# Layer 3 of a four-layer graph-attention kernel: the output additions read a PSUM tile only when it is whole, and the planner has new ranks

## The chip, the cores and the metric

The kernel runs on one core of one Trainium2 chip. The metric is the device time of one execution in microseconds, here the median over several runs of the same program. The work is spread over five engines that run side by side and meet only through semaphores: PE (TensorE, matrix products), DVE (VectorE), ACT (ScalarE), POOL (GpSimd), and SP (SyncE), which issues nearly all transfers.

## The reference, cut to what matters

The input `x` holds 128 graphs of 64 nodes with 512 features, in float32, and `adj` is one 64x64 adjacency mask per graph. Four layers follow each other, each with its own layernorm, a ReLU and a residual:

```python
h = jnp.maximum(_layernorm(x, axis=-1), 0.0)
x = x + _L0_gnn_ref(h, adj, ...)     # and L1, L2: masked attention, 4, 8 and 4 heads
h = jnp.maximum(_layernorm(x, axis=-1), 0.0)
x = x + _L3_gnn_ref(h, adj, ...)     # layer 3, below
```

Layer 3 is another kind of attention, with 8 heads of 64:

```python
m = embs @ map_w.T + map_b                        # "map"
n = sem / norm                                    # rows of m, per head, scaled to length 1
cos_adj = (cos(n, n) * (~sm) > 0.1)
q = m @ q_w.T + q_b ;  k = m @ k_w.T + k_b
p_attn = softmax(where(sm, NEG, q k^T / 8)) * keep
adj = cos_adj * p_attn
sem_h = embs @ gcn_map_w.T + gcn_map_b            # gcn_W is folded into this product ("sem")
out = relu(adj @ sem_h @ gcn_W.T / (adj.sum(-1) + 1))
```

So each output element is the larger of zero and a weighted sum, plus the residual `x`.

## The kernel before, in words

**Tiling.** The 8192 rows of `x` are cut into 16 steps `s` of 512 tokens, which are 8 graphs. Each layer goes over the 16 steps. A product of a 512x512 weight with the 512 tokens of a step is done by a scheme with seven half-size products instead of eight (`winograd`, L789 on, calls `product`, whose matmul is L741). It uses three PSUM tiles in turn, called mA, mB and mC in the profile: mA from one ring of two tiles, mB and mC from another ring of two, which the squared lengths (`mmn`) use as well. ACT reads the first value out of a tile (L758, L762 with a bias, L778) and DVE adds a later one (L771, L782).

**Layer 3, one step.** Four such products are made: `map`, `sem`, `q` and `k`. Beside them there are four blocks of small 64x64 matmuls or of a 32-column product: the scores `sc` (L1090), the cosines `cos` (also L1090), the weighted sums `po` (L1475) and the squared lengths `mmn` (L1033). `sc`, `cos` and `po` each take two PSUM tiles of two banks, called u = 0 and u = 1, and all come from one ring of two such tiles (`r_sc`). A tile is handed on only when all of its readers are done. On the way from `sc` to `po`, DVE masks the scores (L1100), takes the maximum (L1106), subtracts it (L1116); ACT takes the exponential (L1119); DVE sums rows (L1126), makes a 0/1 mask of the cosines (L1428) and multiplies (L1437); POOL divides (L1135); ACT copies 32x32 blocks (L1144) and DVE transposes (L1148). The squares that `mmn` sums are made by ACT (L1028), and the sums are read by DVE (L1013).

**The end of a step.** `last` (L1447 on) issues the `po` matmuls: for each u, first half b = 0 and then half b = 1 of the tile, 16 matmuls each in the source. `finish` (L1342) is the other side: for each half, DVE reads 256 columns out of both banks of the tile, takes the maximum with zero and adds the residual tile `xres` in one instruction (L1349). Then SP stores the sums (L1361; L1356 in the last step). The residual tiles were loaded before (L1334) into a ring of three. In the kernel before, `finish` is started ahead of the matmuls of its tile, and two events (`halves`) tell it that a half is written.

**What sets the order.** Nothing is ordered by hand. A planner (`Order.run`) runs all parts as coroutines against assumed durations, such as `dve(0.69)`, and writes each instruction into its engine's queue when it comes up: the stream that can start first is taken, and among equal starts the one with the lower rank. The ranks come from the table `RANK`, one number for each kind of work and layer; rank 0 is reserved for reading out PSUM tiles, which may also hold back another operation on DVE or ACT that would be in their way. On the chip every engine works through its own queue in the order that the planner wrote. Dependencies between engines are set as the instructions are written, and for PSUM they go by whole banks: a matmul written behind a DVE read of the same bank waits for that read, even if it goes to other columns.

**What else the change touches.** `norms` uses a small tile `rn` for the reciprocal lengths, in a pool with one buffer.

Of the kernel before, what the change touches and what calls it, by code (L numbers as in the profile page):

```python
# [8 lines left out]
F32 = mybir.dt.float32  # L9
# [5 lines left out]
P = 128  # L15
# [16 lines left out]
LEAD = [(0, 0), (0, 1)]  # L32

RANK = {
    "lead": (0.3, 1.5, 5.5, 5),
    "load": (4, 5.5, 1.5, 2),
    "norm0": (1.5, 3.5, 3.5, 6.5),
    "norm1": (4.5, 2.5, 1, 4),
    "move": (6.5, 4.5, 6, 0.3),
    "turn": (1.5, 1, 6, 3.5),  # L40
    "part": (3.5, 3.5, 4, 6),
    "weight": (5.5, 4.5, 5.5, 2.5),
    "proj": (6.5, 5, 5, 6),
    "out": (3.5, 5, 5, 3),
    "front": (2, 3, 0.5, 3),
    "soft": (1.5, 1.5, 0.3, 1),
    "near": (2, 2, 2, 2),
    "trans": (3.5, 1, 0.5, 2),
    "att": (2.5, 0.5, 2, 2),
    "res": (5.5, 6, 1.5, 5.5),  # L50
    "msum": (4.5, 4.5, 4.5, 4.5),
    "length": (4.5, 3.5, 1.5, 5),
}


# [4 lines left out]
def rank(what, l):  # L60

    return Rank(RANK[what][l])
# [28 lines left out]
class Stream:  # L91
# [14 lines left out]
    def quads(self):  # L106
        return self.op[3:] == ("quads",)
# [115 lines left out]
def pe(us):  # L223
    return ("pe", us, 0.25)
# [6 lines left out]
def dve(us):  # L231
    return ("dve", us, 0.1)


def act(us):
    return ("act", us, 0.1)


def pool(us):
    return ("pool", us, 0.15)  # L240


def load(us=2.2):
    return ("sp", 0.6, us)
# [3 lines left out]
def gnn_stack(ctx: ExitStack, tc: tile.TileContext, a: dict, out: bass.AP):  # L248
# [3 lines left out]
    od = Order()  # L252
# [10 lines left out]
    small = ctx.enter_context(tc.tile_pool(name="small", bufs=4))  # L263
    soft = ctx.enter_context(tc.tile_pool(name="soft", bufs=3))
# [617 lines left out]
    st, p_ready, s_ready, p_used, pt_done, o_used, turn = {}, {}, {}, {}, {}, [], []  # L882
# [110 lines left out]
    def sums_after(e, B, z, done, last):  # L993
        yield e

        T, z["T_done"] = yield from (r_w if last else r_t).new("mT_T")
        t2, z["t2_done"] = yield from r_t2.new("mT_T2")
        z["T"] = T = [T[:, 0], T[:, 1], t2, T[:, 2]]
        done.set()
        yield from sums_of_b(B, T, z["T_made"])  # L1000
# [10 lines left out]
    def lengths_out(ss, p_, pe_, done):  # L1011
        yield dve(0.69)
        nc.vector.tensor_copy(ss, p_)  # L1013
        pe_.set()
        done.set()

    def norms(mT, s, m_ready, ready, used):

        yield m_ready
        if s == 0:  # L1020
            yield o_done
        elif s < NG - 1:
            yield lengths[s - 1]
        sqs = []
        for c in range(NC):
            sq, e = yield from r_u.new("sq")
            yield act(0.63)
            nc.scalar.activation(sq, mT[:, c, :], AF.Square)  # L1028
            sqs.append((sq, e))
        p_, pe_ = yield from r_mm.new("mmn")  # L1030
        for c in range(NC):
            yield pe(0.24)
            nc.tensor.matmul(p_[32 * c:32 * (c + 1), :], sel, sqs[c][0], start=True, stop=True)  # L1033
            sqs[c][1].set()
        ss, se = yield from r_u.new("ss")
        copied = od.event()
        od.spawn(lengths_out(ss, p_, pe_, copied), 0)
        yield copied
        d = [dram.tile([8, TB * P], F32, name=f"{n}{s}") for n in ("ss", "rs")]
        yield ("sp", 2.4, 2.2)  # L1040
        for c in range(NC):
            nc.sync.dma_start(d[0][2 * c:2 * c + 2, :], ss[32 * c:32 * c + 2, :])
        se.set()
        if s == NG - 1:
            squares.set()

        rs = small.tile([P, 32], F32, tag="rn", name="rn", bufs=1)
        yield load(2.2)
        nc.sync.dma_start(rs, d[0].rearrange("h (k n) -> (h k) n", n=32))

        yield dve(0.2)
        nc.vector.tensor_scalar_max(rs, rs, 1e-16)
        yield pool(6.0)
        nc.gpsimd.tensor_tensor(rs, rs, mhalf[:, 0:1].to_broadcast([P, 32]), ALU.pow)
        yield load(2.2)
        nc.sync.dma_start(d[1].rearrange("h (k n) -> (h k) n", n=32), rs)
        nr = []

        if s == NG - 2:
            yield squares  # L1060
        for c in range(NC):
            t, e = yield from r_u.new("nr")
            yield ("sp", 1.3, 3.1)
            for par in range(2):
                v = d[1][2 * c + par:2 * c + par + 1, :]
                nc.sync.dma_start(t[par * N:(par + 1) * N, :],
                                  bass.AP(tensor=v.tensor, offset=v.offset,
                                          ap=[[0, N], [1, TB * P]]))
            nr.append((t, e))
        yield used  # L1070
        for c in range(NC):
            t, e = nr[c]
            yield pool(1.3)
            nc.gpsimd.tensor_mul(mT[:, c, :], mT[:, c, :], t)
            e.set()
        ready.set()
# [251 lines left out]
    def last_residuals(s, got):  # L1328
        for u in range(2):
            v, e = yield from r_xres.new()  # L1330
            x3 = v.rearrange("p b (g e) -> p (b g) e", g=2)
            for s2 in range(2):
                yield load(2.8)
                nc.sync.dma_start(x3[s2 * N:(s2 + 1) * N], by_half(x_of(3, s), 2 * u, s2))  # L1334
            got[u] = (x3, e)
            got["e", u].set()

    def by_half(x, t, s2):

        return x[t * P:(t + 2) * P, s2 * H:(s2 + 1) * H].rearrange("(i n) e -> n i e", n=N)  # L1340

    def finish(s, u, po, poe, got, halves):  # L1342
        yield got["e", u]
        x3, xe = got[u]
        for b in range(2):
            yield halves[b]
            v = x3[:, 2 * b:2 * b + 2, :]
            yield dve(0.69)
            nc.vector.scalar_tensor_tensor(v, po[:, :, b * H:(b + 1) * H], 0.0, v,  # L1349
                                           ALU.max, ALU.add)  # L1350
            if s == NG - 1:
                for s2 in range(2):
                    yield load(2.8)
                    q = slice(s2 * H, (s2 + 1) * H)
                    o = out[(s * TB + 2 * u + b) * P:(s * TB + 2 * u + b + 1) * P, q]
                    nc.sync.dma_start(o.rearrange("(i n) e -> n i e", n=N),  # L1356
                                      v[s2 * N:(s2 + 1) * N])
        poe.set()
        for s2 in range(2 if s < NG - 1 else 0):
            yield load(2.8)  # L1360
            nc.sync.dma_start(by_half(out[s * TB * P:(s + 1) * TB * P, :], 2 * u, s2),  # L1361
                              x3[s2 * N:(s2 + 1) * N])
        xe.set()
# [83 lines left out]
    def last(s):  # L1447
        z = st[3, s]
        got = {("e", u): od.event() for u in range(2)}
        od.spawn(last_residuals(s, got), rank("res", 3))  # L1450
        yield p_ready[3, s]
        room = []
        if s < NG - 1:
            for u in range(2):
                yield z["pt_ready", u]
            for u in range(2):
                room.append((yield from r_sc.new("po3")))
        for u in range(2):
            if s == NG - 1:
                yield z["pt_ready", u]  # L1460
                room.append((yield from r_sc.new("po3")))
            pt, pte = z["pt", u]
            po, poe = room[u]
            halves = [od.event() for _ in range(2)]
            od.spawn(finish(s, u, po, poe, got, halves), 0)
            for b in range(2):
                t = 2 * u + b
                for i in range(4):
                    yield quads(0.121)
                    for ch in range(2):  # L1470
                        h = 4 * ch + i
                        c, par = h // 2, h % 2
                        for g in range(2):
                            r = slice(g * N, (g + 1) * N)
                            nc.tensor.matmul(  # L1475
                                po[ch * N:(ch + 1) * N, g, (4 * b + i) * N:(4 * b + i + 1) * N],
                                pt[r, 8 * par + 2 * c + b, :],
                                z["v"][r, t, h * N:(h + 1) * N], start=True, stop=True)
                halves[b].set()
            pte.set()  # L1480
            if u == 1:
                z["v_done"].set()

    def fronts(steps):
        for l, s in steps:
            yield rank("front", l)
            yield from front(l, s)
# [88 lines left out]
```

## Time and profile before

| | before |
|---|---|
| median of 3 runs | 2678.22 us (2678.01 to 2680.61) |
| profiled execution | 2674.79 us |
| its span, first to last instruction | 2673.0 us |
| PE busy | 2629.7 us, 98% of the span |
| DVE, ACT, POOL busy | 72%, 71%, 60% of the span |
| granted PE clock | 0.998 |
| from the first `po` block (1855.63 us) to the end of the span | 817.4 us |

The profile is of one execution, and the runs are of others, so a sum of durations is made against 2673.0 us and then carried over to the median. PE is busy almost throughout, so what counts is what PE waits for and in which stretch. The times of rows in a timeline are microseconds from the start of the span. One float32 matmul of the source is two records of PE: the 32 matmuls of a `po` tile are 64 records, and a block of two tiles is 128.

### The profile page before, as it was taken

What the parts mean: (1) busy time and instruction counts of PE and PEld (TensorE: products, weight loads), DVE (VectorE), ACT (ScalarE), POOL (GpSimd) and SP (SyncE); (2) the same over time, 40 slices, a digit from 0 to 9 for tenths busy, and PEclk for the clock granted to TensorE, in tenths of its full rate; (3) what the DMA queues carried; (4) which work ended last, traced back from release to release, by engine and by line L of the source; (5) the groups of instructions that cost most, each with busy time, mean ns of one, the idle gap of its engine ahead of it and who ended that gap; (6) DMA issues with size and microseconds to landing.
All of it is one profiled execution on the core that took longest, in us unless ns stands there. A gap on an engine that the chain in (4) does not pass through costs nothing.

```text
span 2673.0 us, 64016 instructions
## 1 busy us (share of the span) xinstructions
PE 2629.7 (98%) x26352; PEld 2308.0 (86%) x26352; DVE 1918.9 (72%) x2843; ACT 1890.3 (71%) x3508; POOL 1608.8 (60%) x1246
## 2 busy tenths in 40 slices
PE   8999999999999999999999999999999999999998
PEld 7888988888888888888899999888888888888887
DVE  6877878876677667758767777658666677766667
ACT  5677777888777877876667777766676666677654
POOL 5776767554444435445767777786665566565563
PEclk9999999999999999999999999999999999999999
DMA  6666663221122112115656666332223332222231
GB/s 177 154 168 144 175 146 118 93 96 49 49 65 80 49 55 75 64 49 129 162 130 177 152 168 160 118 103 66 66 68 83 95 79 66 66 65 74 75 82 48
DMA packets 414004, 270.02 MB, mean 101 GB/s; under 512 B 277520, under 2 KB 322576, under 8 KB 413712
## 3 DMA queue, kind: packets, MB, share of 16 engines
q1 hardware_dynamic: 402048, 254.40, 35.0%
q10 hardware_dynamic: 11664, 11.54, 1.4%
q8 instruction: 207, 3.39, 0.5%
q14 instruction: 85, 0.70, 0.1%
HBM read 166.77 MB, written 67.63 MB: 88 GB/s over the span
## 4 chain that ended last, share of the span: by engine, by line
PE 92%; DVE 3%; DMA 2%; issue 1%; SPq 1%; ACT 1%; POOL 1%; POOLq 0%; DVEq 0%
PE mA L741 47%; PE mC L741 24%; PE mB L741 12%; PE sc L1090 3%; PE po L1295 2%; DMA xin<-x 1%; PE cos L1090 1%; PE po L1475 1%; SPq L1361 1%; PE mmn L1033 1%; DVE xres L1349 1%; PE mP L741 1%; DVE sc L1100 0%; POOL v L1006 0%; PE ptr L688 0%
## 5 line engine op out<-in xcount | busy, mean ns | idle before, releaser
L1144 ACT COPY F<-E 32x512 f32<-32x512 f32 x752 | 462.5, 615 | 37.5 <-POOL E L1135 25.6
L1232 POOL TENSOR_TENSOR xres<-xres,u 128x512 f32<-128x512 f32 x192 | 253.0, 1323 | 352.4 <-ACT u L1227 289.5
L515 ACT ACTIVATE xin<-xin,rs 128x512 f32<-128x512 f32 x320 | 248.8, 810 | 11.5 <-DVE rs L508 9.3
L1211 POOL TENSOR_TENSOR xres<-xres,u 128x512 f32<-128x512 f32 x192 | 249.8, 1319 | 5.6 <-DVE qk L782 4.1
L611 ACT COPY hT<-xin 32x512 f32<-32x512 f32 x390 | 240.1, 616 | 6.5
L497 DVE BATCH_NORM_STATS2 st<-xin 128x6 f32<-128x512 f32 x320 | 213.0, 668 | 40.9 <-DMA xin<-x 33.2
L506 POOL TENSOR_TENSOR rs<-rs,mhalf 128x2 f32<-128x2 f32 x160 | 120.1, 751 | 171.9 <-DVE rs L504 157.1
L758 ACT COPY v<-mA 128x256 f32<-128x256 f32 (+1 forms) x192 | 92.0, 479 | 131.6 <-PE mA L741 124.2
L385 POOL TENSOR_TENSOR t<-hT,t 128x512 f32<-128x512 f32 x126 | 178.4, 1416 | 4.8
L1126 DVE TENSOR_REDUCE sm<-E 128x16 f32<-128x1024 f32 x124 | 149.6, 1206 | 18.4 <-ACT E L1112 15.1
L1135 POOL TENSOR_TENSOR E<-E,sm 128x1024 f32<-128x1024 f32 x64 | 122.5, 1920 | 61.3 <-DVE sm L1130 42.1
L385 POOL TENSOR_TENSOR t<-hT 128x512 f32<-128x512 f32 x63 | 82.9, 1316 | 123.7 <-DVE hT L621 111.6
L1100 DVE COPY_PREDICATED sc<-n,negs 128x1024 f32<-128x1024 uint8 x64 | 99.8, 1559 | 57.5 <-PE sc L1090 57.2
L1148 DVE STREAM_TRANSPOSE F<-F 128x1024 f32<-128x1024 f32 x94 | 116.2, 1236 | 29.1 <-ACT F L1144 29.0
L741 PE MATMUL mA<-w_vo,t 128*128 128x128 f32 (+1 forms) x768 | 135.2, 312 | 1.5 <-ACT v L758 1.0
L1112 ACT ACTIVATE E<-sc,mx 128x64 f32<-128x64 f32 x512 | 123.9, 332 | 17.1 <-DVE mx L1109 17.0
L1227 ACT COPY u<-mA 128x512 f32<-128x512 f32 x144 | 84.4, 586 | 64.3 <-PE mA L741 55.8
L741 PE MATMUL mA<-hT,w_qk 128*128 128x256 f32 x496 | 126.1, 382 | 3.3 <-DVE hT L662 3.1
L1135 POOL TENSOR_TENSOR E<-E,f 128x1024 f32<-128x1024 f32 x30 | 61.1, 2036 | 104.9 <-DVE nz L1180 57.2
L741 PEld LDWEIGHTS mA<-w_vo,t 128*128 128x128 f32 x768 | 112.8, 191 | 11.4 <-ACT v L758 1.2
L741 PE MATMUL mA<-t,w_qk 128*128 128x256 f32 x496 | 119.7, 379 | 0.0
L1106 DVE TENSOR_REDUCE mx<-sc 128x16 f32<-128x1024 f32 x96 | 116.9, 1218 | 2.5
(236 smaller groups left out, 7341.4 us busy)
## 6 DMA issues: line engine op xcount, KB each, us to landing
x<-xres SPq DMA_DIRECT2D x96, 512.0 KB
xin<-x SPq DMA_DIRECT2D x96, 512.0 KB
xres<-x SPq DMA_DIRECT2D x64, 512.0 KB
F<-xin SPq DMA_DIRECT2D x480, 64.0 KB
xres<-in_x SPq DMA_DIRECT2D x32, 512.0 KB
u<-rs SPq DMA_DIRECT2D x128, 128.0 KB
xres<-x SPq DMA_DIRECT2D x64, 256.0 KB
xin<-in_x SPq DMA_DIRECT2D x30, 512.0 KB
```

The costliest lines, as they stand in the source:

```text
L385: nc.gpsimd.tensor_tensor(o, i0, i1, ALU.subtract)
L497: nc.vector.bn_stats(st, v[:, t, :])
L506: nc.gpsimd.tensor_tensor(rs[:, 0, :], rs[:, 1, :], mhalf[:, :2], ALU.pow)
L515: nc.scalar.activation(v[:, t, :], v[:, t, :], func, bias=rs[:, 2, t:t + 1], scale=rs[:, 0, t:t + 1])
L611: nc.scalar.copy(o, v)
L741: nc.tensor.matmul(o, l, r, start=(first and m == 0 and k == 0), stop=(k == KC - 1), skip_group_check=True)
L1112: nc.scalar.activation(E[:, i, :], S3[:, i, :], AF.Exp, bias=mx[:, i:i + 1], scale=0.125)
L1126: nc.vector.tensor_reduce(o, E, AX.X, ALU.add)
L1135: (nc.vector if vector else nc.gpsimd).tensor_mul(E, E, sm[:, :, None].to_broadcast([P, 16, N]))
L1144: nc.scalar.copy(F[g * N + 32 * k:g * N + 32 * (k + 1), :, 32 * i:32 * (i + 1)], E[g * N + 32 * i:g * N + 32 * (i + 1), :, 32 * k:32 * (k ...
L1211: nc.gpsimd.tensor_add(xr[:, t, :], xr[:, t, :], bo[l])
L1232: nc.gpsimd.tensor_add(v, v, both(u))
```

## The change

Three edits are made.

1. In `last`, `finish` is started after the matmuls of its whole tile, not before them, and the two `halves` events are gone. The four additions (L1348 in the changed kernel) and the stores (L1360, L1355) are the same instructions as before.
2. Most numbers of `RANK` are new.
3. The pool of `rn` has two buffers.

```diff
 RANK = {
-    "lead": (0.3, 1.5, 5.5, 5),
-    "load": (4, 5.5, 1.5, 2),
-    "norm0": (1.5, 3.5, 3.5, 6.5),
+    "lead": (0.5, 1, 5.5, 5),
+    "load": (2.5, 4, 4.5, 2),
+    "norm0": (1.5, 3.5, 4, 6.5),
     "norm1": (4.5, 2.5, 1, 4),
-    "move": (6.5, 4.5, 6, 0.3),
-    "turn": (1.5, 1, 6, 3.5),
-    "part": (3.5, 3.5, 4, 6),
-    "weight": (5.5, 4.5, 5.5, 2.5),
-    "proj": (6.5, 5, 5, 6),
-    "out": (3.5, 5, 5, 3),
-    "front": (2, 3, 0.5, 3),
-    "soft": (1.5, 1.5, 0.3, 1),
-    "near": (2, 2, 2, 2),
-    "trans": (3.5, 1, 0.5, 2),
-    "att": (2.5, 0.5, 2, 2),
-    "res": (5.5, 6, 1.5, 5.5),
-    "msum": (4.5, 4.5, 4.5, 4.5),
-    "length": (4.5, 3.5, 1.5, 5),
+    "move": (2.5, 4.5, 6, 4.5),
+    "turn": (0.5, 1, 6, 3.5),
+    "part": (2, 3, 2.5, 6),
+    "weight": (6, 4.5, 3, 2),
+    "proj": (5.5, 5, 5, 6),
+    "out": (4.5, 5, 5, 6.5),
+    "front": (2, 4, 0.5, 3),
+    "soft": (1.5, 2.5, 0.3, 4.5),
+    "near": (2, 5.5, 4.5, 2),
+    "trans": (3.5, 1, 0.5, 1),
+    "att": (2.5, 2, 1.5, 6),
+    "res": (4.5, 6, 2, 5.5),
+    "msum": (1.5, 1.5, 1.5, 1.5),
+    "length": (3, 3.5, 6.5, 5.5),
 }
...
-        rs = small.tile([P, 32], F32, tag="rn", name="rn", bufs=1)
+        rs = small.tile([P, 32], F32, tag="rn", name="rn", bufs=2)
...
-    def finish(s, u, po, poe, got, halves):
+    def finish(s, u, po, poe, got):
         yield got["e", u]
         x3, xe = got[u]
         for b in range(2):
-            yield halves[b]
             v = x3[:, 2 * b:2 * b + 2, :]
             yield dve(0.69)
...
             po, poe = room[u]
-            halves = [od.event() for _ in range(2)]
-            od.spawn(finish(s, u, po, poe, got, halves), 0)
             for b in range(2):
...
-                halves[b].set()
             pte.set()
             if u == 1:
                 z["v_done"].set()
+            od.spawn(finish(s, u, po, poe, got), 0)
```

What the planner makes of it can be read from the order of the built programs. On PE the two programs are the same in layers 0 to 2 and in layer 3 up to and with the first block of `po`. From there on, in a step of the steady part (`q` and `k` below belong to one step, and `map` and `sem` to the next):

```
before:  q x7  k x4  po  k x3  map x1 (3 of 4)  sc  map x7  sem x1 (2 of 4)  cos  sem x2  mmn  sem x5
after:   q x7  k x7  po  map x2 (1 of 4)  sc  map x6  sem x3 (2 of 4)  cos  sem x1  mmn  sem x4
```

Here "x4" means four of the seven half-size products, and "(3 of 4)" tells after which matmul of a product the small block cuts in; the number behind it counts the rest of that product as one. Around these, ACT, DVE, POOL and SP have another order in layer 3: after `sc`, ACT reads mC of `map` (L762) before the first exponential (L1119), where it came behind it; DVE takes the statistics of the next input (L497) behind the first masked and subtracted tile, where they came before it; the two halves of the next input (L569) are each loaded behind one pair of output stores, where both came behind all four; POOL normalises `m` (L1074) in one run of four. In layers 0 to 2 a few neighbours change places on DVE, ACT, POOL and SP.

## The prediction

> **What bounds the kernel now.** I read the page's busy times and chain first, then PE's waits, then one steady step of layer 3 on PE and on the engines that PE waits for.
>
> ```profile
> PE 2629.7 (98%) x26352; PEld 2308.0 (86%) x26352; DVE 1918.9 (72%) x2843; ACT 1890.3 (71%) x3508; POOL 1608.8 (60%) x1246
> ...
> PE 92%; DVE 3%; DMA 2%; issue 1%; SPq 1%; ACT 1%; POOL 1%; POOLq 0%; DVEq 0%
> ```
>
> PE is the bound; the amount of PE work does not change, so only PE's idle time can be won or lost. The list of what PE waits for (total, times, longest) says where it is:
>
> ```profile
> PE po L1475 <- DVE xres L1349: 13.1, 16, 0.8
> PE ptr L688 <- ACT xin L515: 8.8, 1, 8.8
> PE mC L741 <- ACT m L762: 5.3, 6, 1.7
> ```
>
> The second row is the start of the kernel, before the first input is there. The first and third are in layer 3. In the timeline of PE, one step (start, length, what, and in brackets the wait before it):
>
> ```profile
> 2125.01 1.04 PE L1475 MATMUL po<-v,F 64*64 64x64 f32 x56
> 2126.87 1.28 PE L1475 MATMUL po<-v,F 64*64 64x64 f32 x72 [0.81 <-DVE xres L1349]
> 2128.08 1.99 PE L741 MATMUL mA<-mT_T,w_k 128*128 128x256 f32 x8
> ...
> 2134.75 2.10 PE L1090 MATMUL sc<-kT,qT 64*64 64x64 f32 x128
> 2136.78 0.70 PE L741 MATMUL mA<-hT,w_map 128*128 128x256 f32 x2
> ...
> 2144.86 1.99 PE L741 MATMUL mC<-hT,w_map 128*128 128x256 f32 x8 [0.48 <-ACT m L762]
> ```
>
> The `po` matmuls stop near the end of their first tile until DVE has read its first half. With the break they take 2128.08 - 2125.01 = 3.07 us; the 128 records of `sc`, of the same shape, take 2136.78 - 2134.75 = 2.03 us without one. So the break costs 1.04 us, more than the 0.81 shown as idle, as PE also runs empty and fills again. The other row is a late reading of mC, and the timelines of ACT and DVE say why:
>
> ```profile
> 2143.02 1.06 ACT L1119 ACTIVATE E<-E 128x1024 f32<-128x1024 f32 x1 [1.21 <-DVE E L1116]
> 2143.98 0.82 ACT L762 ACTIVATE m<-mC,vecs 128x256 f32<-128x256 f32 x2
> ```
> ```profile
> 2137.44 0.69 DVE L497 BATCH_NORM_STATS2 st<-xin 128x6 f32<-128x512 f32 x1 [2.63 <-DMA xin<-x]
> 2138.05 1.95 DVE L1100 COPY_PREDICATED sc<-adj,negs 128x1024 f32<-128x1024 uint8 x1
> ```
>
> ACT's queue has the exponential ahead of mC; the exponential waits for DVE's subtraction, which is late because DVE's queue had to wait for an input transfer ahead of masking the scores.
>
> **What the Trainium skill says.** "PSUM — Partial Sum Buffer", section "PSUM bank collisions raise a hardware error", says that two engines may not touch one bank and quadrant at once, even at different columns, and that PSUM has to be guarded by bank. That is the wait above: the two halves of a `po` tile are columns of the same two banks, and the trace agrees (16 waits, 0.81 us each). The section "Engine vs sequencer instructions" there says that the ACT, DVE and POOL queues are strictly first in, first out; the trace agrees, as mC's reading stands behind an exponential that is not ready. "SBUF — State Buffer", section "Who interferes with whom", says that a DVE instruction with two SBUF inputs contends with POOL's reads; the trace has L1437 at 1.23 us with POOL idle and at 1.95 to 2.05 us beside it, so DVE's times depend on what stands beside them.
>
> **The change, part by part.**
>
> *No break in `po`.* `finish` now stands behind the whole tile in the program, so no matmul of this tile is written behind a DVE read of its banks; the next tile is in other banks. Steps 0 to 13 have one break each: 14 x 1.04 = -14.6 us. The last two steps are counted below.
>
> *Where the stall could go.* `sc` comes next in the ring, so it waits for the four additions. Let `po` end at T. DVE takes 1.29 us for two additions. The first pair can start once the first tile is written, at T - 1.0 plus the 0.24 us from PE to DVE that the trace shows: -0.75 to +0.55; the second to +1.85. PE has a product of `map` (1.73 us) and a quarter of the next (0.43) in between, so `sc` comes up at T + 2.2 for its first tile and T + 3.2 for its second. Margin 1.3 us or more. The additions stand behind the additions to `kT` on DVE, which are over by about T - 2.9. Cost 0; if that cover is gone, each us is lost 13 times. What stands behind the additions on DVE, the transposes of `hT` (2.36 us, to sc - 0.35 + 2.36 = sc + 2.0), is for the next step and has a whole step of time.
>
> *Reading mC of `map`.* With DVE free at sc + 2.0: masking 1.95, addition 0.65, maximum 1.2, subtraction 1.2, so the exponential can start at sc + 7.0. mC's product ends then too; ACT reads it at 7.2 to 8.05, and PE wants it back at 8.7. The wait no longer depends on DVE. Its price before: `sc` to `sc` is 57.25 us in clean steps (2192.75 to 2250.00) and 57.99, 59.22, 58.00, 59.20, 57.99, 57.99 in the six with the wait, together 6.9 us more. -6.9 us.
>
> *The input transfers.* A half of xin was landed 5.1 to 7.2 us after its issue (2189.34 to 2194.41; 2304.11 to 2311.33). Now the first half is issued behind two stores of about 0.9 us, at sc + 0.2, so lands at 5.3 to 7.4; its statistics come up on DVE at 7.0. At most 0.4 us late, and what follows (second masking to 10.5, second subtraction to 15.4) is due when `cos` wants its second tile, at 17.4. Cost 0, cover 2 us.
>
> *Squares and `mmn`.* On ACT, after the last `map` reading at 13.25: two normalisations (0.8 each), one `sem` reading, one square, the exponential 1.06, three squares, to 19.1. `mmn` comes up at 19.6. Cost 0 in the steady steps with only 0.4 us of cover; in the first step after the split, where `mmn` and `cos` are mixed, I allow +0.9 us. DVE reads `mmn` at 22, as before (2156.06 - 2134.75 = 21.3), so the chain over SP, POOL's power (5.43 us) and the `u<-rs` loads keeps its time. POOL's second division ends at about 35 against 31.7, but `po` is 6.7 us later in the step.
>
> *`sc` of step 14.* Before, it took 2599.61 - 2596.83 = 2.78 us with a wait for `kT`; now two products stand in between. -0.7 us.
>
> *The tail.* `sem` of step 15 now ends before `po` of step 14, so POOL's row additions are out of the way. But DVE's four additions (2.5 us) come just before the last row sum and division, which are ready at 2660.7 on the clock of before against 2659.5; the last transposing, `po`, additions and eight stores (6.35 us of issuing, from 2663.93 before) follow it. +1.0 us.
>
> *Ranks in layers 0 to 2.* PE's order is the same and PE is 99.9% busy from 460 to 1000 us and 99.7% from 1000 to 1500; DVE's swapped pairs are shorter than 2 us and have slack: 0, between -0.5 and +1. The second `rn` buffer matters only where two steps overlap, at the end: 0.
>
> Sum: -14.6 - 6.9 - 0.7 + 0.9 + 1.0 = -20.3 us. The span becomes 2652.7 us, the profiled execution 2654.5, and the median, 3.4 us above it before, 2658.
>
> **The rivals.**
>
> *Half of it comes back (chance 0.10).* The squares are late: the cover of `mmn` is 0.4 us. If the second subtraction comes 1.2 us later than worked out, `mmn` waits 0.8 us in 12 steps, about +10 us: 2668. For it: planner times for DVE are shorter than the trace's (masking 1.5 against 1.95). Against it: POOL is idle during L1437 now, so DVE runs faster there.
>
> *The stall only moves (0.04).* `sc` waits as long for the additions as `po` did. It takes additions 1.3 + 1.0 us late, for example an added 1.23 us transpose and a late residual tile. Then only the mC part is won, or less: within 0.2%, 2674.
>
> *Slower (0.04).* The same place, from 1.3 + 1.5 = 2.8 us late the step is longer than before. Should residual loads (L1334), of which three now stand behind the stores and inputs, hold the additions for 4 us, 13 x (4 - 2.8) = +16 us: 2694. Against it: they are issued some 45 us ahead of their use.
>
> The change not doing what it says is excluded as far as order goes: in the built program the wait in mid-tile is gone.
>
> **How the numbers follow.** The main course has 0.82 and a range of its own of 2652 to 2664: the lower end takes in shorter breaks elsewhere and a free tail, the upper one 0.4 us in each step. Reaching to most of the first rival gives 2651 to 2668 for 8 in 10. A measurement of this kernel can tell about 0.2%, 5.4 us, from no change. Faster: 0.82 + 0.10 = 0.92; within: 0.04; slower: 0.04.
>
> **What would show it.** PE's list of waits has no `po <- DVE xres` in the middle of the layer, and the `po` block takes 2.03 us. `sc` to `sc` is about 56.2 us. mC has no wait for L762. Wrong, if `sc`, `cos` or `mmn` show waits of 0.5 us or more in most steps, if steps are 57 us or longer, or if layers 0 to 2 end later (first `po` block at 1855.6 us).

## The result, and the profile after

The changed kernel takes 2668.3 us (median of 5 runs, 2663.12 to 2670.35), the kernel before 2679.51 us beside it (2678.01 to 2680.7). The ratio is 0.9955, with a 95% interval from 0.994 to 0.9969: faster by about 11 us, half of the 20.3 us of the sum. The median is 0.3 us above the upper end of the stated range (2668); by the ratio, which is 2666.2 us against the 2678.22 of the prediction, it is just inside. A second series gave 2668.67 us and 0.9963 (0.9949 to 0.9977).

The page and the list of what PE waited for, of the changed kernel:

```profile
PE 2628.4 (99%) x26352; PEld 2308.2 (87%) x26352; DVE 1901.6 (71%) x2843; ACT 1888.6 (71%) x3508; POOL 1594.1 (60%) x1246
...
PE 93%; DVE 2%; DMA 2%; issue 1%; POOL 1%; ACT 1%; SPq 0%; DVEq 0%; POOLq 0%; ACTq 0%
```
```profile
PE ptr L688 <- ACT xin L515: 8.9, 1, 8.9
PE mA L741 <- POOL t L385: 6.3, 1, 6.3
PE mA L741 <- ACT v L758: 2.9, 4, 1.0
```

PE is still the bound with the same work. The waits of `po` (13.1 us) and of mC (5.3 us) are gone, as forecast. Two rows are new: one wait of 6.3 us for POOL near the start, and one for ACT's reading of `v`, in `sem`. One step on PE's timeline:

```profile
2240.51 2.09 PE L1472 MATMUL po<-v,F 64*64 64x64 f32 x128
...
2244.89 2.10 PE L1090 MATMUL sc<-kT,qT 64*64 64x64 f32 x128
...
2258.67 1.89 PE L741 MATMUL mB<-w_sem,hT 128*128 128x256 f32 x8
2261.30 1.13 PE L741 MATMUL mA<-w_sem,t 128*128 128x256 f32 x4 [0.74 <-ACT v L758]
...
2265.53 1.54 PE L1033 MATMUL mmn<-u,sel 128*32 128x512 f32 x8
2267.01 1.99 PE L741 MATMUL mC<-w_sem,t 128*128 128x256 f32 x8
```

The `po` block has no break and takes 2.02 us (to 2242.53), and `sc` waits for nothing. But two places further on are late: `sem`'s third product, and `mmn`, which takes 1.48 us until the next product instead of 1.07 in a clean step. DVE and ACT in the same step say why:

```profile
2255.50 0.69 DVE L497 BATCH_NORM_STATS2 st<-xin 128x6 f32<-128x512 f32 x1 [3.84 <-DMA xin<-x]
...
2257.32 1.23 DVE L1100 COPY_PREDICATED sc<-adj,negs 128x1024 f32<-128x1024 uint8 x1
2258.45 0.69 DVE L782 TENSOR_TENSOR m<-m 128x512 f32<-128x512 f32 x1
```
```profile
2259.23 0.84 ACT L762 ACTIVATE m<-mA,vecs 128x256 f32<-128x256 f32 x2 [4.96 <-DVE m L782]
2259.96 0.81 ACT L515 ACTIVATE xin<-xin,rs 128x512 f32<-128x512 f32 x1
2260.67 0.58 ACT L758 COPY v<-mA 128x512 f32<-128x512 f32 x1
```

DVE's queue stands for 3.84 us at the statistics of an input that has not landed. Behind them are `m`'s sum, behind that ACT's last reading for `m`, then one normalisation, then the reading of `v` that PE wants. The prediction put this wait at 0.4 us or less.

Which transfer is it? The input of a step comes in two halves, each a transfer of its own. SP's lines show when they are issued, and DVE takes statistics once more 8 us later, without a wait:

```profile
2243.05 1.31 SPq L1360 DMA_DIRECT2D out<-xres  x2
2244.47 1.86 SPq L569 DMA_DIRECT2D xin<-x  x1
2246.43 1.26 SPq L1360 DMA_DIRECT2D out<-xres  x2
2247.74 1.11 SPq L569 DMA_DIRECT2D xin<-x  x1
```
```profile
2263.84 0.68 DVE L497 BATCH_NORM_STATS2 st<-xin 128x6 f32<-128x512 f32 x1
```

The trace also holds the semaphore that each instruction waits for, and the times of its updates, 16 for each transfer. The statistics at 2255.50 wait for semaphore 107. That one belongs to the second half, issued at 2247.74; its 16th update came at 2255.48, 7.74 us after the issue. The first half, issued at 2244.47, had landed at 2249.94, after 5.47 us. It is the one that DVE takes at 2263.84 (semaphore 104). So the half that was there waited behind the half that was not.

In the table, "middle" runs from the second `sc` block of layer 3 to the last one (the steps without the start and the end), all from one profiled execution each; the last column is the median over the timed runs.

| kernel | first `sc` of layer 3 at | middle | last `sc` to end | median |
|---|---|---|---|---|
| before | 1799.95 | 784.45 | 45.1 | 2679.51 |
| changed | 1802.64 | 770.03 | 47.5 | 2668.3 |
| difference | +2.7 | -14.4 | +2.4 | -11.2 |

The forecast for the middle was -21.3 us (breaks 14.6, mC 6.9, step 14 0.7, less 0.9), for the start 0 and for the end +1.0. So 6.9 us are missing in the middle, 2.7 at the start and 1.4 at the end: 11.0 of the 20.3 us.

### The profile page after: what moved, and what is told of

It is laid out like the page before. It is cut to its first block, busy times and chain, and to the rows that moved or that the text cites. A ratio compares the mean times of both kernels' runs of the same rounds, so it can differ in the third digit from the quotient of the medians.

```text
span 2663.7 us, 63997 instructions
## 1 busy us (share of the span) xinstructions
PE 2628.4 (99%) x26352; PEld 2308.2 (87%) x26352; DVE 1901.6 (71%) x2843; ACT 1888.6 (71%) x3508; POOL 1594.1 (60%) x1246
## 4 chain that ended last, share of the span: by engine, by line
PE 93%; DVE 2%; DMA 2%; issue 1%; POOL 1%; ACT 1%; SPq 0%; DVEq 0%; POOLq 0%; ACTq 0%
PE mA L741 48%; PE mC L741 24%; PE mB L741 12%; PE sc L1090 3%; PE po L1295 2%; PE cos L1090 1%; DMA xin<-x 1%; PE po L1472 1%; PE mmn L1033 1%; PE mP L741 1%; PE ptr L688 0%; DVE xres L1348 0%; DVE st L497 0%; DVE sc L1100 0%; SPq L1360 0%
## 5 line engine op out<-in xcount | busy, mean ns | idle before, releaser
L497 DVE BATCH_NORM_STATS2 st<-xin 128x6 f32<-128x512 f32 x320 | 213.3, 669 | 44.2 <-DMA xin<-x 34.9
L741 PEld LDWEIGHTS mA<-w_vo,t 128*128 128x128 f32 x768 | 112.8, 191 | 11.5 <-ACT v L758 1.2
L762 ACT ACTIVATE m<-mA,vecs 128x256 f32<-128x256 f32 x96 | 40.2, 470 | 113.6 <-PE mA L741 80.0
```

The lines of the kernel that those rows point to most:

```text
L497: nc.vector.bn_stats(st, v[:, t, :])
L741: nc.tensor.matmul(o, l, r, start=(first and m == 0 and k == 0), stop=(k == KC - 1), skip_group_check=True)
```

## The experiments

**Three first questions: the edit without the ranks, the start, the late input.** Four kernels ran beside each other; the kernel before had 2678.57 us there.

*1. The edit alone.* `RANK` as before, the edit of `finish` and the second `rn` buffer as in the changed kernel.

> The edit of `finish` alone, with the old ranks in all four layers (so the second residual load of the start goes out behind 11 of the 16 F transfers as before, and in layer 3 the four stores, both halves of the input and the four residual loads go out one after the other as before). In its order of instructions the weighted sums still stand inside the unit of `k`, some 7.5 us ahead of the scores, so the whole additions can be over (2.5 us after the last `po`) before the additions to kT that follow them on VectorE are due. Theory (the edit alone takes the break away, the new ranks cost 3 us in layer 0 and about 7 us in layer 3 by late input): no break in `po` in 13 or 14 steps, -14.6 us against before, so 2664 us, the start as before (first layer-3 `sc` at 1800), faster than the 2668 of the changed kernel by 3 to 5. Rival (new ranks are what hides the additions): the additions come late, kT's additions behind them, `sc` waits 1 to 1.7 us in each of 13 steps, 2674 to 2680.

Measured: 2669.27 us (2665.63 to 2674.55), ratio 0.9964 (0.9953 to 0.9975). Neither the theory (2664 us) nor the rival (2674 to 2680) had it. No `po` waits, as the theory says, and nothing is late at `sc`; yet it isn't faster than the changed kernel. Its list of waits between 1850 and 2600 us begins with

```profile
PE mC L741 <- ACT m L762: 10.8, 10, 2.9
```

In the kernel before, the same row has 5.3 us in 6 times in this stretch. Where mC was just in time before, it is late by 0.48 us in six steps and by more in four: counted from the start of `po`, PE asks for it 1.04 us earlier, but the input is issued only some 0.6 us earlier (5.9 to 6.2 us after that start, not 6.3 to 6.7). The plain step is 56.95 us long, not 56.21. The chain of this kernel's step from 2078 us, the middle left out (start, length, what), begins with the input:

```profile
2075.07 5.92 DMA xin<-x
...
2081.63 1.25 DVE sc L1100
...
2084.72 1.14 DVE E L1116
...
2085.89 1.06 ACT E L1119
2086.94 0.74 ACT m L762 x2
...
2087.72 1.99 PE mC L741 x8
```

With the old ranks DVE takes the half that is issued first (2075.07 here, landed at 2080.99). So mC's wait and the changed kernel's wait for `v` could have one cause, an input half later than its place in DVE's queue. The new ranks do not take it away, they change the half and what it hits. (Its profile is of its slowest run, so the waits of its median run may be smaller.)

*2. One rank of the start put back.*

```diff
-    "move": (2.5, 4.5, 6, 4.5),
+    "move": (6.5, 4.5, 6, 4.5),
```

> The changed kernel with one number put back: the rank of `move` in layer 0, 2.5 to 6.5. On SP's queue only one thing changes place, the second residual load of the start goes out behind 11 instead of 16 F transfers; on VectorE only a few instructions of layers 0 and 1 change places. Theory (the start is lost by this load): GpSimd's wait of 2.49 us for `xres` and TensorE's wait of 6.3 us for GpSimd's t shrink to the 3.1 us for VectorE's hT that before had, first layer-3 `sc` about 1799.5 to 1800, total 2665 us against the 2668.3 of the changed kernel (-3). Rival (the 2.7 us come from many small shifts of layers 0 to 2): 2668, with the start still 1802 to 1803.

Measured: 2665.64 us (2664.39 to 2666.21), ratio 0.9953 (0.994 to 0.9966), first `sc` of layer 3 at 1800.65. On POOL's timeline (start, length, line, and in brackets the wait before it) the wait is in the changed kernel, in the first fence, and absent with the rank put back, in the second:

```profile
64.41 2.49 POOL L1211 TENSOR_TENSOR xres<-xres,u 128x512 f32<-128x512 f32 x2 [8.08 <-DMA xres<-in_x]
```
```profile
56.81 3.65 POOL L1211 TENSOR_TENSOR xres<-xres,u 128x512 f32<-128x512 f32 x2
```

The theory's mechanism is there: POOL waits 7.6 to 8.8 us for this load in the six profiles with the new rank, and 0.5 us at most in the seven with the old one. The time fits it by the medians (-2.7 us against 2668.3), less so by the ratios (0.9953 against 0.9955, about 0.5 us), as the kernel before was 0.9 us faster here. And the profiled start of experiment 1, with the old rank, was at 1804.91, so one execution says little; experiment 7 tests it again.

*3. The planner told another landing time for the inputs of layer 3.*

```diff
-                    yield load(3.9)
+                    yield load(3.9 if l < 3 else 9.0)
```

> The changed kernel with one number of the planner: it is told that an input transfer of layer 3 takes 9.0 us to land instead of 3.9. The transfers keep their order on SP's queue in the steady steps; on VectorE the statistics of the first half of the input move behind the second masking and the sums of `m` that they held up. Theory (the late landing costs only because VectorE's queue stands behind it): the statistics wait 0.3 us or less instead of 2 to 3.8, no step between two first scores is over 56.6 us, the twelve steps give back 5 to 7 us, total 2661 to 2663. Rival (the transfers themselves, 16 engines full, are what is late, and what needs the input is late with it wherever it stands): no gain, 2667 to 2669.

Measured: 2675.44 us (2674.06 to 2678.94), ratio 0.9989 (0.9981 to 0.9997). As a whole the expectation failed by 13 us. The steps from `sc` to `sc` say where: from the second on they take 73.15, 58.36, 56.08, 56.73, 56.12, 56.13, 56.59 us and so on, so the steady ones are as the theory has them, and the second is 14 us too long. There the planner made another order, and `po` met late work on DVE:

```profile
1865.10 1.99 PE L1472 MATMUL po<-v,F 64*64 64x64 f32 x64 [6.04 <-DVE rn L1052]
1924.57 1.16 PE L1472 MATMUL po<-v,F 64*64 64x64 f32 x64 [1.78 <-DVE E L1116]
1929.78 1.99 PE L1472 MATMUL po<-v,F 64*64 64x64 f32 x64 [4.05 <-DVE rs L508]
```

The stops cost more than the idle time. After the first of them the same matmuls are slower for a while:

```profile
1867.02 3.51 PE L741 MATMUL mA<-w_sem,hT 128*128 128x256 f32 x8
1870.37 1.89 PE L741 MATMUL mB<-w_sem,hT 128*128 128x256 f32 x8
```

The granted clock in the trace is 0.50 for 6.83 us there (1863.30 to 1870.13), and for another 6.83 us at the last of the three stops (1928.15 to 1934.98). The experiment cannot decide between theory and rival, since the short steps come after a long stop.

*4. The input's transfers first.*

```diff
         poe.set()
+        if 2 <= s < NG - 5:
+            yield l_ready[3, s + 5, 1]
         for s2 in range(2 if s < NG - 1 else 0):
...
-                    yield load(3.9)
+                    yield load(3.9 if l < 3 else 6.0)
```

> The changed kernel with the transfers of a steady step of layer 3 put in another order: both halves of the next input ahead of the four stores and of the last two residual loads (the stores wait until they are issued), and the planner told 6.0 us for their landing, which keeps the statistics on VectorE ahead of the second masking as in the changed kernel. Theory (half 0 is late because a store stands ahead of it and three or four other transfers share its engines): it lands 5 to 7 us after its issue instead of 10 to 11, the statistics wait under 0.5 us, 4 to 7 us less, 2661 to 2664; the stores end later, which nothing waits for. Rival (landing is set by the total in flight, not by the order): landing 9 us or more, 2667 to 2669.

Measured: 2677.87 us (2676.13 to 2681.85), ratio 0.9998 (0.9989 to 1.0006). It failed in the same way: 73.52 and 58.99 us for the second and third step, then 56.0 to 56.4 in all but one of the steady ones. The "10 to 11" us of its expectation, and the "9.7 to 11" of experiment 11, are no landing times: they run from the issue of the first half to the landing of the second. By the semaphores, in the eight steady steps of the changed kernel the first half lands 5.1 to 6.8 us and the second 6.7 to 8.3 us after its own issue.

**Second question: is the late input the cause?** The change to the planner was limited to inputs from step 7 of layer 3 on, so that the first steps stay as they are. The kernel before had 2678.43 us here.

*5. The changed kernel again.*

> The changed kernel as it is, run beside the next three on one chip. Expected 2666 to 2669 us, with its start (first layer-3 `sc`) near 1802.6 as in the three profiles of this order of instructions so far (1802.64, 1802.75, 1802.75).

Measured: 2668.67 us (2667.31 to 2671.27). First `sc` of layer 3 was at 1803.98, 1.4 us later than said, and there are six waits for `v` instead of four, together 5.0 us.

*6. The landing told from step 7 on.*

```diff
-                    yield load(3.9)
+                    yield load(9.0 if l == 3 and s >= 7 else 3.9)
```

> The changed kernel, but for the inputs from step 7 of layer 3 on the planner is told that they take 9.0 us to land instead of 3.9 (the trial with 9.0 for all of layer 3 had steady steps of 56.1 us, but also another order in the first three steps, where `po` waited 12 us). The first steps of layer 3 are in the order of the changed kernel here. Theory (the late input costs only because VectorE's queue stands behind its statistics): the steps between first scores from the fifth on take 56.1 to 56.6 us as in that trial, 5 to 6.5 us less than the changed kernel on the same chip. Rival (that trial's steady steps were short because its start was long, the sixteen engines having caught up): steps of 56.9 to 57.7 as in the changed kernel, no gain.

Measured: 2659.81 us (2657.21 to 2660.69), ratio 0.9928 (0.9914 to 0.9942), 8.9 us under the changed kernel beside it, more than the 5 to 6.5 that were said; the steps from the fifth to the twelfth take 56.08 to 56.33 us. No long stop comes ahead of them, so the rival is out. DVE's timeline in one of them:

```profile
2247.45 1.22 DVE L1100 COPY_PREDICATED sc<-adj,negs 128x1024 f32<-128x1024 uint8 x1
...
2250.18 0.69 DVE L782 TENSOR_TENSOR m<-m 128x512 f32<-128x512 f32 x1 [0.25 <-ACT m L778]
...
2251.90 0.68 DVE L497 BATCH_NORM_STATS2 st<-xin 128x6 f32<-128x512 f32 x1
```

In these steps the transfers are issued in the same order as in the changed kernel, and the second half, for which these statistics wait here too, is no earlier: it lands 8.8 to 10.6 us after the start of `sc`, against 9.2 to 10.6. But `m`'s sum is no longer behind it, and DVE comes to the statistics at 11.1. The planner also moved other instructions on DVE, ACT and POOL, and `mmn` on PE; the cleaner test is experiments 9 and 10. The middle is 763.01 us, 21.4 less than before; the forecast for it was 21.3.

*7. That, and the rank of `move` back at 6.5.*

> As the last one (9.0 us told from step 7 of layer 3 on), and the rank of `move` in layer 0 back at 6.5. Theory (two separate losses): another 2 to 3 us less than with the planner's number alone, first layer-3 `sc` at 1800 to 1800.7. Rival (the start varies from execution to execution by as much, whatever the rank: the profile of the edit with the old ranks began 3 us late too): within 1 us of the kernel with the planner's number alone, over the five rounds.

Measured: 2657.3 us (2656.25 to 2659.37), ratio 0.9922 (0.9907 to 0.9938), 2.5 us under experiment 6, with first `sc` at 1800.47, as said. Together with experiment 2 the rank of `move` costs some 2.5 us by the medians. But the intervals of experiments 6 and 7 overlap, and so do the profiles, where first `sc` blocks are between 1801.24 and 1803.98 with the new rank and between 1799.95 and 1804.91 with the old one. The wait of POOL is shown; its price is likely, not clear of noise.

*8. That, and the end relieved.* The residual inputs of the last step are loaded one step earlier, the second one into a free buffer of `xin`.

```diff
     def last_residuals(s, got):
         for u in range(2):
-            v, e = yield from r_xres.new()
+            if s == NG - 1 and u == 1:
+                v, e = yield from r_xin.new("xlast")
+                v = v[:, 0:2, :]
+            else:
+                v, e = yield from r_xres.new()
...
```

> As the last one, and the end of the kernel relieved: the residual inputs of the last step are loaded one step earlier, the second of them into a free buffer of `xin` instead of the buffer whose store of the step before has to land first. Theory (the end of the changed kernel waits 3.7 us on VectorE for that load, with TensorE already done 3 us before): the last additions follow the last `po` within 1.5 us, from the last `sc` to the end 44 to 45 us instead of 47.5, total 2.5 to 3.5 us less than the last one. Rival (the stores at the end set it: eight stores after the last addition, whenever the load lands): less than 1 us.

Measured: 2654.99 us (2653.65 to 2656.35), ratio 0.9911 (0.9896 to 0.9927), 2.3 us under experiment 7. From the last `sc` to the end it takes 45.7 us, after 47.9. The last additions on DVE, in the changed kernel and then here:

```profile
2656.27 1.89 DVE L1348 SCALAR_TENSOR_TENSOR xres<-po,xres 128x512 f32<-128x512 f32 x3 [3.68 <-DMA xres<-x]
```
```profile
2646.49 0.69 DVE L1358 SCALAR_TENSOR_TENSOR xlast<-po,xlast 128x512 f32<-128x512 f32 x1 [0.24 <-PE po L1488]
```

In the changed kernel PE is done at 2653.27, and the end waits for a residual load issued at 2651.06, because its buffer is free only when a store of the step before is through. The gain is a bit under what was said, as the stores at the end remain; the two intervals overlap, the single runs hardly.

**Third question: what are the ranks and the edit worth with the input out of the way?** The kernel before had 2678.08 us here.

*9. The edit alone, with the landing told from step 6 on.* Experiment 1 with `load(9.0 if l == 3 and s >= 6 else 3.9)`. By the two traces one instruction per step changes its place, the first statistics of an input on DVE; the order on PE, ACT, POOL and SP is the same.

> The edit of `finish` with the old ranks (2669.3 us before), and the planner told 9.0 us for the landing of the inputs from step 6 of layer 3 on. One instruction per step moves, the first statistics of an input on VectorE, from ahead of the first masking to some 36 instructions later; no other engine's order changes. Theory (one cause for both: the statistics wait on VectorE for the late input, and what stands behind them, `m`'s sums and maskings, makes TensorE wait at mC or for ScalarE's v): the mC waits from 2030 us on (10.8 us in 10 steps) are gone, steps of 56.2 us, 8 to 13 us less than the edit alone, 2656 to 2661. The new ranks are then worth nothing beside it. Rival (the mC waits come from the place of the sums of `m` on VectorE in the old ranks, or from ScalarE's work): the steps stay at 56.95 to 58.2, 2668 to 2670.

Measured: 2655.87 us (2655.78 to 2656.77), ratio 0.9921 (0.9907 to 0.9935), 13.4 us under experiment 1 by the medians of the two series and 11.5 by the ratios, at the upper end of what was said. From the third to the fourteenth the steps take 56.1 to 56.2 us but for one of 56.43, and between 1850 and 2600 us PE waits nowhere but 0.2 us before one `sc`. One moved instruction per step takes away all of mC's waits, so their cause is that DVE stood at a late input ahead of other work, and the new ranks are not needed.

*10. The kernel before, with the landing told from step 6 on.*

> The kernel before, with nothing of the change, and the planner told 9.0 us for the landing of the inputs from step 6 of layer 3 on: the same one instruction per step moves on VectorE. Theory: the mC waits of `map` go (in the profile of before six steps lay 0.7 to 2.0 us above 57.25, 6.9 us in all), the breaks in `po` stay (1.04 us in each step), steps of 57.25 us, 2671 to 2673. Rival (those waits are ScalarE's or of the order of the sums): no change, 2678.

Measured: 2669.84 us (2667.58 to 2671.58), ratio 0.997 (0.9959 to 0.9981). In its list of waits between 1850 and 2600 us mC is gone and `po` is left:

```profile
PE po L1475 <- DVE xres L1349: 11.8, 14, 1.2
PE sc L1090 <- ACT kT L762: 0.2, 1, 0.2
```

Every step from the third to the twelfth takes 57.25 us. Against experiment 9 that is 1.04 us per step, and 2669.84 - 2655.87 = 14.0 us in the runs.

*11. The transfers' order, from the fourth step on.* The edit of experiment 4 with `3 <= s`, and the planner's 3.9 us as in the changed kernel. What follows from it on DVE and ACT, and the place of `mmn` on PE, changes too.

> The changed kernel with the transfers alone in another order, from the fourth step of layer 3 on: both halves of the input ahead of the four stores and of three of the four residual loads; the planner keeps its 3.9 us, so the statistics stand even earlier on VectorE and their start shows when the half has landed. Theory (a store ahead of it and the transfers that share the engines are what makes the half late): the first half lands 5 to 7 us after its issue instead of 9.7 to 11, steps of 56.4 us or less, 3 to 6 us less than the changed kernel on the same chip (2663 to 2666). Rival (its landing is set by the total in flight): 9 us or more, and as the statistics stand in front of more work, steps of 58 us or more, 2670 to 2680.

Measured: 2660.81 us (2659.99 to 2664.94), ratio 0.9942 (0.9929 to 0.9956), by the ratios 5.6 us under the changed kernel of the second series; the steps from the third to the twelfth take 56.0 to 56.4 us but for one of 57.67, in which `sc` waits 1.4 us for something that the profile does not name. SP's and DVE's lines for that step:

```profile
2183.68 0.89 SPq L569 DMA_DIRECT2D xin<-x  x2
2184.61 0.61 SPq L1334 DMA_DIRECT2D xres<-x  x1
2185.32 4.26 SPq L1362 DMA_DIRECT2D out<-xres  x4
```
```profile
2191.75 0.68 DVE L497 BATCH_NORM_STATS2 st<-xin 128x6 f32<-128x512 f32 x1
```

By their semaphore these statistics too are of the second half, issued at 2184.10 and landed at 2190.86. In the eight steady steps it is issued 1.7 us before the start of `sc`, right behind the first half, where it was issued 2.2 to 2.9 us after it in the changed kernel. It takes 4.7 to 8.0 us to land (6.7 to 8.3 there), so it is there 3.0 to 6.3 us after the start of `sc`, not 9.2 to 10.6. On the mean of eight steps that is 5.4 us earlier, of which 4.0 are the earlier issue. So most of the cure is the place of the second half in SP's queue; the rest of the landing, and the other order on DVE and ACT, were not tried apart.

## Why the prediction was half right

*No break in `po` (-14.6):* right. Experiments 9 and 10 differ by the edit of `finish` (and the buffer of `rn`), and give 14.0 us and 1.04 us per step.

*Where the stall could go (0):* right. `sc` waited for the additions in no step; the rival "the stall only moves" is out.

*Reading mC (-6.9):* the wait went away and its size was about right (experiment 10 gains 8.2 us, experiment 6 brings the middle to 21.4 where 21.3 was forecast). The prediction named its first link, 2.63 us of waiting for an input, and took a later place of the statistics on DVE as the cure. With the place, the half changed as well, and DVE waits for an input again.

*The input transfers (0, "at most 0.4 us late", "cover 2 us"):* this is the step that failed, and not by its durations. DVE comes to the statistics 6.8 us after the start of `sc` in seven of the eight steady steps (7.5 in the other), where 7.0 was said; the half that is issued first has landed by then, 4.7 to 6.4 us after that start, where 5.3 to 7.4 was said. But the prediction took for granted that the statistics in this place are those of the half that is issued first. That is so in the kernel before. In the changed kernel, in all eight steady steps, they wait for the semaphore of the half that is issued second, behind the other two stores, and it lands 9.2 to 10.6 us after the start of `sc`. DVE stood for 2.0 to 3.8 us, where 0.4 at most was said.

The length of the steps shows that this is all of it. Take the time from the start of one `sc` to the start of these statistics, and add 47.16 or 47.17 us: that is the start of the next `sc`, in 23 of the 24 steady steps of three executions (the changed kernel, experiment 5 and experiment 2; in the other step it is 47.40). Three of them:

| step of the changed kernel from | statistics start after `sc` | to the next `sc` | difference |
|---|---|---|---|
| 2131.62 | 9.20 | 56.37 | 47.17 |
| 2074.06 | 10.40 | 57.56 | 47.16 |
| 2244.89 | 10.61 | 57.78 | 47.17 |

So each us that the second half lands later makes the step one us longer. With the 56.1 us of an undisturbed step in experiment 6 this begins 8.9 us after the start of `sc`, so even the cover of some 2 us was right. What stands behind the statistics is the second masking, and behind it `m`'s sum for ACT, whose in-order queue then has a normalisation ahead of the `v` that PE wants. The price is the 6.9 us that are missing in the middle (8.9 us between experiments 5 and 6), where 0 was said.

Why DVE takes the second half first is not shown. In the code the halves are normalised by two streams, `norm0` and `norm1`, whose ranks in layer 3 are 6.5 and 4 in both kernels. Where the planner believes both halves to have landed, the second one would come first. By the numbers above, the first half in this place would not have been late; exchanging the two was not tried.

*Squares and `mmn` (0, cover 0.4 us):* 0.4 us was lost there in five of the eight steps from 2017 us on, as the squares stand behind the same ACT work. So the rival "half of it comes back" named the right total (2668) and one of the places, but as its cause slow work on DVE, not the input. The range reached up to 2668 only for the sake of this rival, so that it meets the measured time is luck.

*First step after the split (+0.9) and `sc` of step 14 (-0.7):* right in direction. The step of 59.57 us became 59.20, which is +0.67 beside the break; the last step and a half went from 88.25 to 85.59 us, -2.7, of which 1.04 are the break, so the rest is -1.6, not -0.7.

*The tail (+1.0):* the direction was right, the size 2.4, and the reason was another. The prediction counted DVE's order; PE ends in time, and the last additions wait for a residual load (experiment 8).

*Ranks in layers 0 to 2 (0, between -0.5 and +1):* wrong at one place. PE's order is the same, but layer 0 starts with transfers. There one load, moved behind five more transfers on SP, is issued at 59.45 instead of 52.18 us, and POOL, whose queue keeps its order, waits for it ahead of the sums that PE needs. Likely price: some 2.5 us (experiments 2 and 7).

*The slower rival* named late residual loads (L1334). None held the additions in a steady step, but in the last step one did.

*The second `rn` buffer (0):* not tried alone.

What was needed is smaller than what was changed: the edit of `finish` and one later landing time told to the planner (2655.87 us) are within noise as good as the new ranks with three repairs (2654.99), and better than the changed kernel by 9 to 13 us (by ratios and by medians).

## What to carry to other kernels

A wait has a front and a cause: where PE waits for ACT, ACT for DVE and DVE for a transfer, a reordering moves the front, and the transfer can still be late for somebody. So follow each wait back to its first link, and there ask what stands behind it in an in-order queue.

At that link, ask which transfer it is. Two halves of one tile have one name in the profile, but each has its own issue and its own semaphore, and a new order can exchange them. A landing time counted from the wrong issue (9.7 to 11 us in two of the expectations above, where it was 6.7 to 8.3) looks like a slow transfer and hides the repair that may be nearest.

A late input is cheap where nothing urgent stands behind it: statistics placed later on DVE gave 8 to 13 us here. But a planner that is told late landing times from the first step on can also make a worse order: in experiment 3 the second step of layer 3 became 14 us longer.

## What the runs showed of the hardware that was not expected

- A short stop of PE costs a constant on top of the idle time that the profile shows: 0.81 us shown cost 1.04, 0.48 cost 0.74 (a step of 56.95 against 56.21), 1.70 cost 1.96 (58.17). It is 0.23 to 0.26 us each time.
- A longer stop also costs clock. In the 13 profiles, behind the first 20 us, every stop of PE of 2.9 us or more while it still had work goes with a granted clock of 0.50 for one to three times 3.41 us; after single stops of 1.4 to 2.3 us the clock stayed at 1.00. In experiment 1 a stop of 2.92 us made a step of 61.08 us, 4.87 more than 56.21: the stop, the constant of 0.25, and half of 3.41 us at half the clock. The matmuls behind it, of which eight take 1.89 us elsewhere:

```profile
2263.46 2.78 PE L741 MATMUL mC<-hT,w_map 128*128 128x256 f32 x8 [2.92 <-ACT m L762]
2266.03 2.83 PE L741 MATMUL mA<-t,w_map 128*128 128x256 f32 x8
```

- Two gains with one cause can be more than their sum. The edit alone gave 9.3 us, the landing time alone 8.2, both together 22.2: without the break PE ran into more of the late input (10.8 us of waits instead of 5.3). The surplus of 4.7 us by medians, 3.5 by ratios, is not clear of the intervals of the three runs.
- The issuing lines of SP are no measure of a landing. "Perfetto Trace Analysis" of the Trainium skill, section "Per-instruction lifecycle: what the profiler-reported window actually captures", says that a transfer's data movement lies outside the window shown; the trace agrees: L569 is shown at 0.7 to 1.9 us in the steady steps, while the halves land 5.1 to 8.3 us after its start.
- The start varies from execution to execution: with the same order of instructions in layers 0 to 2, the first `sc` of layer 3 came at 1799.95 us in the kernel before and at 1804.91 in experiment 1, whose five F transfers of layer 0 behind the residual load took SP 10.27 us to issue instead of 7.42. PE's stop near 65 us was longer too (4.79 us, not 3.14), and the granted clock was 0.50 for 6.83 us, not 3.41. With the old rank of `move`, the three profiles with 3.41 us have first `sc` at 1799.95 to 1800.65, the four with 6.83 us at 1801.30 to 1804.91.
